# A block of S5 and attention on one core: other products between the last pairs, and x's store at another place in the queues

## The chip, the cores and the metric

The kernel runs on one core of a Trainium2 chip, as one launch. The metric is the device time of a whole execution in microseconds. A core has five engines, each with its own instruction queue: TensorE (PE in the profile; its weight loads are PEld), VectorE (DVE), ScalarE (ACT), GpSimd (POOL) and SyncE (SP), which here does little but start DMAs. Matrix products land in PSUM, eight banks of 128 x 512 f32; all else is in SBUF or in DRAM.

## The reference

Two layers run one after the other on x of shape (2, 2048, 512), each modulated by a condition vector of 512 per batch. The first is an S5 block: layer norm and modulation, a diagonal complex state space of 128 states scanned along the 2048 positions, a gated residual, and a feed-forward part. The second is multi-head attention (16 heads of width 32) whose layer norm takes its gain and offset from the condition.

```python
h = ln(y) * (1 + scale_a) + shift_a
y = y + gate_a * s5(h)                      # 2 Re(C scan(Lam, B h)) + D h
h = (ln(y) * (1 + scale_c) + shift_c) * (1 + scale_f) + shift_f
y = y + gate_f * (gelu(h @ W1 + b1) @ W2 + b2)
h = gamma(c) * (ln(y) * g + b) + beta(c)
q, k, v = split(h @ Wqkv.T + bqkv)
y = y + softmax(q k.T / sqrt(32)) v @ Wp.T + bp
```

W1 is 512 x 2048, W2 is 2048 x 512, Wqkv is 1536 x 512, all f32. (The sketch leaves out how the condition's shifts, scales and gates are made.)

## The kernel before

The kernel has a first part, up to about 1308 us, and then the attention. The first part walks through eight chunks of 512 rows, four of each batch, in the order `order`. Every chunk goes through the S5 layer, the feed-forward layer (ff) and the products for k, q and v; these are stored to DRAM (`kd`, `qd`, `vd`), and x with the bias of the output projection is stored to `x2` for the attention.

Chunk 0's ff is computed plainly: 16 hidden blocks, each `ff_first` (4 matmuls and a gelu) and `ff_second` (4 matmuls). In its shadow POOL makes, with `combine` (L784 to 796), the sums of weight blocks that a seven-product scheme (Strassen's in Winograd's form) needs, and SP stores them to DRAM as `w1d`, `w2d`, `wkd`, `wvd`. What is done beside which block is written down in a table `due`.

Chunks 1 to 7 are turns of a loop. In a turn, `now` is the chunk whose ff is computed, `behind` the one before it, whose q, k and v are made, and `ahead` the one after it, which goes through S5. The turn has four stretches on TensorE:

1. *ff pairs*: `pairs_of` with 8 pairs (products at L909). A pair is seven products of 4 matmuls, 128 x 256 each: 0, 1, 4, 2, then the previous pair's product 6, then 3 and 5. Between them, ScalarE copies a half bank (`za`, L926), VectorE makes sums (`za`, `zb`, L927 to L943), and ScalarE applies gelu (`hidden`). Then come the two input products of S5 for `ahead` (`s5_in`, `pu`, L530, 8 matmuls of 128 x 512 each).
2. *FF-out*: `whole_of` with depth 8 (L962), seven products of 32 matmuls in the order 0, 1, 2, 3, 5, 4, 6. After product 2 stand the output products of S5 (`s5_out`, `pa`, L576).
3. *q/k pairs*: `pairs_of` with 4 pairs, over sums of blocks that `at_sums` has POOL make (`parts`, L874 to 877).
4. *v*: `whole_of` with depth 2.

Work of the other engines is put between the products by lists: `beside[n]` is issued after step n of `pairs_of` (two steps a pair) or after product n of `whole_of`. The schedule is manual: each engine, and SP's DMA starting too, executes its instructions in the order in which the program issues them. An instruction that waits holds back all that follows it on its engine.

Some helpers are spread over those lists. `norm_steps` gives a layer norm as rows (statistics, L144, a row each), a scale (13 small VectorE operations, L149 to L133) and a normalisation (L154). `block_steps` gives a transpose in two steps: 32 x 32 turns on VectorE (L460), and a `move` of 16 DMAs on SP (L467). After the move ScalarE's `features` (L477) apply the modulation. `at_rows` (L625 to 634) adds the projection's bias to x's rows on POOL (L627) and stores them with four DMAs on SP (L634). `load_x` (L222) loads the rows of the chunk after `ahead`, into one of three buffers in rotation, which is the buffer of `behind`. `gated_in` (L1105 to 1116) adds FF-out's quarters to x, and `bias` (L1140) adds the second ff bias for `ahead`. `ff_features` are `ahead`'s features for the next turn's ff; one stands in each of the q/k pairs' steps 3 to 6.

Weights come through a ring of four 1 MB slots (`wk`, `wq`, `wv`, `w3`). `more` (L855 to 865) starts the next load on SP after a product has used a slot up; the stream is, a turn, eight loads of w1d, seven of w2d, four of wkd and two of wvd. Eight landing counters are used in rotation by the DMAs that an engine starts, so a DMA also waits for the one eight before it.

After the loop three weights are loaded again for the last chunk's v, k and q (`wkqv`, L1210 to 1214), which is computed plainly with the first heads' attention.

Of the kernel before, what the change touches and what calls it, by code (L numbers as in the profile page):

```python
# [8 lines left out]
F32 = mybir.dt.float32  # L9
# [30 lines left out]
def tile_s5_block_then_sln_attention(  # L40
# [482 lines left out]

    def s5_in(b, c):
        uT = fts.pop((b, c))
        bu = []
        for w in (bT_re, bT_im):
            pu = ones.tile([P, CH], F32, name="pu")
            for k in range(KC):
                nc.tensor.matmul(pu, w[:, k, :], uT[:, k, :], start=k == 0, stop=k == KC - 1)  # L530
            bu.append(pu)
        bus[b, c] = bu

# [78 lines left out]
    def ff_out(b, c):  # L612
        xc, po = xt[b, c], pos.pop((b, c))
        for t in range(TT):
            g = work1.tile([P, D], F32, name="gated")
            nc.vector.tensor_mul(g, po[:, t, :], gate[b, "gate_f"])
            nc.gpsimd.tensor_tensor(xc[:, t, :], xc[:, t, :], g, ALU.add)
# [165 lines left out]

    def combine(block, to, *shape):  # L784

        for at, tag in ((1, "hi"), (5, "lo")):
            pair = work1.tile([P, 2, HC], F32, name="sums", tag=tag)
            views = [pair[:, m, :].rearrange("p (k f) -> p k f", k=shape[0]) for m in range(2)]
            if at == 1:
                nc.gpsimd.tensor_tensor(views[1], block(1, 0), block(1, 1), ALU.add)  # L790
                nc.gpsimd.tensor_tensor(views[0], views[1], block(0, 0), ALU.subtract)
                s2 = views[0]
            else:
                nc.gpsimd.tensor_tensor(views[0], block(0, 0), block(1, 0), ALU.subtract)
                nc.gpsimd.tensor_tensor(views[1], block(0, 1), s2, ALU.subtract)
            nc.sync.dma_start(to(at, at + 2), pair)
# [20 lines left out]
    def by_rows_w2(q):  # L817

        def block(i, j):
            return w2_sb[j][:, q : q + 1, HC * i : HC * i + HC]  # L820

        def to(m0, m1):
            return w2d[m0:m1, :, q, :].rearrange("m p e -> p m e")

        combine(block, to, 1)

# [27 lines left out]

    def more():  # L855

        n = begun[0]
        if n == total:
            return
        begun[0] += 1  # L860
        tag = slots[n % 4]
        src, size = stream[n]
        w = (strip if tag == "w3" else wlate).tile([P, FH * HC], F32, name="wring", tag=tag)
        nc.sync.dma_start(w[:, :size], src)
        ready.append(w)
# [27 lines left out]
    def bank():  # L893
        return psq.tile([P, CH], F32, name="pp")

    def pairs_of(n, x, shape, take, beside):

# [21 lines left out]
        for c in range(n + 1):  # L919
            if c < n:  # L920
# [7 lines left out]
                product(p1, w, 4, t4, 0, True, False)  # L928
                product(p1, w, 2, t1, 1, False, False)
            if c:  # L930
                product(pps[c - 1][1], ws.pop(c - 1), 6, x22, 1, False, True)
                more()
                za, (_, p1) = zas.pop(c - 1), pps.pop(c - 1)
                nc.vector.tensor_tensor(za[:, 0, :], p1[:, HC:], za[:, 0, :], ALU.add)
                take(c - 1, 0, 1, za[:, 0, :])
# [14 lines left out]

    def whole_of(depth, weights, x, take, beside):

        a0, a1, b1, b0 = bank(), bank(), bank(), bank()
        u = strip.tile([P, CH], F32, name="u", tag="u")
        v = strip.tile([P, CH], F32, name="v", tag="v")
        z = strip.tile([P, CH], F32, name="z", tag="z")

        def product(m, out, start, stop):
# [8 lines left out]
            if last:  # L967
                more()

        def run(m):  # L970
            for what, *args in beside.get(m, ()):
                what(*args)

        product(0, a0, True, False)
        nc.scalar.copy(u, a0)
# [21 lines left out]
        take(0, 1, u)  # L997

    for i, now in enumerate(order[:1]):

# [30 lines left out]
        for n in range(3):  # L1031
            due[13, 1].append((more,))

# [20 lines left out]
    for i, now in enumerate(order):  # L1054
# [17 lines left out]

        beside = {n: [] for n in range(-1, 2 * FH + 2)}
        if ahead:
            rows, scale, to = norm_steps(*ahead)
            turns, move = block_steps(*ahead, tag_of(*ahead), by_way=True)
            if new:
                beside[0] += [(s5_gates, ahead[0])]
                beside[6] += [(gate_row, ahead[0], "gb2", gate_b2)]
            beside[0] += rows[:2]  # L1080
            beside[1] += rows[2:3]
            beside[2] += rows[3:]
            beside[4] += scale
            beside[6] += to[:2]
            beside[8] += to[2:]
            beside[10] += turns[:3]
# [68 lines left out]
        whole_of(FH, weight, operand, gated_in, beside)  # L1155
        blocked.pop(now, None)
# [22 lines left out]
        pairs_of(KC, parts_of["at"], 1, heads, beside)  # L1179
        if not ahead:  # L1180
            continue

        vw = [ready.pop(0), ready.pop(0)]

# [3 lines left out]

        parts = parts_of["at"]
        xv = {0: parts[0], 1: parts[1], 2: parts[2], 3: parts[3], 4: parts[4], 5: parts[5], 6: parts[6]}  # L1190

        def operand_v(m, q, t):
            return xv[m][:, q, 0, t * P : t * P + P]

# [667 lines left out]
```

## Time and profile before

Three runs took 3343.62, 3346.92 and 3352.35 us, median 3346.92.

| | us |
|---|---|
| profiled execution, its time | 3344.9 |
| its span, first to last instruction | 3343.0 |
| TensorE busy (mean granted clock 0.986) | 3192.0 |
| first part: start to the first pair | 0 to 212.88 |
| loop of seven turns | 212.88 to 1282.64 |
| last chunk's v, then attention | 1291.12 to 3343 |
| HBM traffic, mean over the span | 119 GB/s |

An entry of the profile names the line in the kernel, the engine, the operation, what is written from what is read, partitions x elements, and a count. Where an engine stood idle before it, brackets give for how long and which instruction or DMA ended that. SPq entries are SyncE's starting of DMAs, whose time includes waits in between when several are put together in one entry.

### The profile page before, as it was taken

The page shows a single profiled execution, that of the slowest core. Times are in us where ns is not written, and L with a number is a line of the kernel's source. Part 1 is how long each engine was busy: PE and PEld are TensorE (multiplying, and loading weights), DVE is VectorE, ACT ScalarE, POOL GpSimd, SP SyncE. Part 2 cuts the span into 40 slices and gives each one's busy share as a digit, 9 for nine tenths or more (in the row PEclk, how much of TensorE's full clock was granted, in tenths as well). Part 3 has the DMA queues.
Part 4 walks back from the last instruction along what each step waited for, and adds up shares of the span by engine and source line. Part 5 has one row for each costly group of instructions (what it writes and reads, how often), then busy time and mean ns, then how long its engine had stood idle before and what let it go on. Part 6 is the DMA issues. An engine that isn't in the chain of part 4 may idle for free.

```text
span 3343.0 us, 38784 instructions
## 1 busy us (share of the span) xinstructions
PE 3192.0 (95%) x12900; PEld 1771.2 (53%) x12900; DVE 2452.6 (73%) x3200; ACT 2014.8 (60%) x2391; POOL 2412.2 (72%) x1464
## 2 busy tenths in 40 slices
PE   7989999999999998999999999999999999999996
PEld 4457878777877885444444444444444444443432
DVE  5246565666657434788888888888888888888884
ACT  2111313121212122699999999999888988888862
POOL 2857363545445332599989999999999999999986
PEclk9999999999999999999999999999999999999998
DMA  8555656566574755323231323133243243233233
GB/s 302 180 191 177 211 182 210 184 202 207 175 228 157 220 188 188 103 62 73 69 73 48 74 67 74 50 76 77 59 99 87 68 97 86 74 85 84 66 101 96
DMA packets 298013, 422.19 MB, mean 126 GB/s; under 512 B 98712, under 2 KB 195224, under 8 KB 286678
## 3 DMA queue, kind: packets, MB, share of 16 engines
q1 hardware_dynamic: 297814, 419.72, 43.5%
q8 instruction: 102, 1.67, 0.2%
q14 instruction: 97, 0.79, 0.1%
HBM read 309.38 MB, written 87.94 MB: 119 GB/s over the span
## 4 chain that ended last, share of the span: by engine, by line
PE 46%; DVE 18%; ACT 17%; POOL 5%; issue 4%; DMA 3%; SPq 2%; ACTq 0%; DVEq 0%; POOLq 0%
PE pp L909 13%; PE o L1358 10%; PE s L1289 8%; DVE run L1305 8%; ACT x L1300 7%; PE pp L962 7%; ACT x L1348 5%; ACT pT L1348 4%; DVE pT L1343 3%; PE py L1441 3%; DVE run L1309 2%; SPq L467 2%; PE pu L530 1%; PE pt_run L1317 1%; PE pk L646 1%
## 5 line engine op out<-in xcount | busy, mean ns | idle before, releaser
L1337 POOL TENSOR_TENSOR x<-x,shift 128x1024 f32<-128x1024 f32 x704 | 1653.4, 2391 | 133.8 <-DMA shift<-flat 109.1
L1289 PE MATMUL s<-qs,ks 128*128 128x512 f32 x2688 | 823.4, 427 | 39.3 <-DVE run L1305 24.8
L1300 ACT COPY x<-s 128x1024 f32<-128x1024 f32 x704 | 692.0, 1011 | 141.6 <-PE s L1289 133.4
L1305 DVE TENSOR_TENSOR run<-s,run 128x1024 f32<-128x1024 f32 x576 | 705.0, 1224 | 74.6 <-ACT x L1300 29.0
L1348 ACT ACTIVATE x<-x 128x1024 f32<-128x1024 f32 x704 | 738.2, 1058 | 19.2 <-POOL x L1337 18.9
L1358 PE MATMUL o<-x,v 128*64 128x512 f32 x2816 | 717.8, 612 | 0.0
L1289 PEld LDWEIGHTS s<-qs,ks 128*128 128x128 f32 x2688 | 444.6, 189 | 454.4 <-DVE run L1305 155.8
L1343 DVE TENSOR_TENSOR pT<-s,shift 128x1024 f32<-128x1024 f32 x320 | 388.8, 1215 | 50.3 <-PE s L1289 50.3
L1309 DVE TENSOR_TENSOR run<-s,run 128x1024 f32<-128x1024 f32 x320 | 389.1, 1216 | 9.5 <-PE s L1289 8.9
L1348 ACT ACTIVATE pT<-pT 128x1024 f32<-128x1024 f32 x320 | 339.4, 1061 | 76.5 <-DVE pT L1343 76.3
L909 PE MATMUL pp<-parts,wring 128*128 128x256 f32 x1344 | 329.8, 389 | 16.1 <-POOL parts L875 15.4
L1358 PE MATMUL o<-pT,v 128*64 128x512 f32 x1280 | 329.3, 593 | 6.6 <-ACT pT L1348 6.6
L1358 PEld LDWEIGHTS o<-x,v 128*64 128x64 f32 x2816 | 157.2, 136 | 309.4 <-issue 250.6
L962 PE MATMUL pp<-wring,h 128*128 128x256 f32 x1344 | 293.3, 379 | 0.0
L909 PEld LDWEIGHTS pp<-parts,wring 128*128 128x128 f32 x1344 | 261.8, 196 | 57.5 <-POOL parts L875 17.8
L909 PE MATMUL pp<-fT,wring 128*128 128x256 f32 x1008 | 251.2, 382 | 26.7 <-DVE zb L943 17.4
L962 PEld LDWEIGHTS pp<-wring,h 128*128 128x128 f32 x1344 | 255.6, 190 | 39.6 <-issue 5.7
L909 PEld LDWEIGHTS pp<-fT,wring 128*128 128x128 f32 x1008 | 190.3, 191 | 60.4 <-DVE zb L943 23.0
L1070 POOL TENSOR_TENSOR h<-h 128x256 f32<-128x256 f32 x56 | 42.5, 758 | 230.2 <-ACT h L1068 218.8
L1358 PEld LDWEIGHTS o<-pT,v 128*64 128x64 f32 x1280 | 91.3, 137 | 191.3 <-issue 141.1
L1305 DVE TENSOR_TENSOR run<-s,x 128x1024 f32<-128x1024 f32 x64 | 78.4, 1225 | 121.6 <-ACT x L1300 121.6
L477 ACT ACTIVATE fT<-moved,s_shift,s_scale 128x512 f32<-128x512 f32 x28 | 20.5, 803 | 217.3 <-DMA moved<-fT 153.8
(360 smaller groups left out, 3173.2 us busy)
## 6 DMA issues: line engine op xcount, KB each, us to landing
wring<-w1d SPq DMA_DIRECT2D x56, 896.0 KB
wring<-w2d SPq DMA_DIRECT2D x49, 1024.0 KB
ks<-kd SPq DMA_DIRECT2D x128, 256.0 KB
qs<-qd SPq DMA_DIRECT2D x512, 64.0 KB
shift<-flat SPq DMA_DIRECT2D x64, 512.0 KB
wring<-wkd SPq DMA_DIRECT2D x28, 896.0 KB
moved<-fT SPq DMA_DIRECT2D x224, 64.0 KB
x<-in_x SPq DMA_DIRECT2D x8, 1024.0 KB
```

Source lines behind the costliest of these rows:

```text
L467: nc.sync.dma_start(moved[32 * g : 32 * g + 32, :, a * P : (a + 1) * P], turned[32 * a : 32 * a + 32, :, g, :],)
L909: nc.tensor.matmul(to, w[:, m, k, :], moving, start=start and k == 0, stop=stop and k == 1, skip_group_check=True,)
L962: nc.tensor.matmul(out[:, t * HC : t * HC + HC], x(m, q, t), w[:, q, :], start=start and q == 0 and t == 0, stop=stop and q == depth - 1 a ...
L1289: nc.tensor.matmul(s[:, e, :], kst[pair_of[n], e][:, kt * P : (kt + 1) * P], qst[n][:, e, :], start=True, stop=True,)
L1300: nc.scalar.copy(x, s)
L1305: nc.vector.tensor_tensor(runs[n], s, kept[n, 0] if kt == 1 else runs[n], ALU.max)
L1309: nc.vector.tensor_tensor(runs[n], raw_scores(n, kt), runs[n], ALU.max)
L1337: nc.gpsimd.tensor_tensor(x, x, shifts[n], ALU.add)
L1343: nc.vector.tensor_tensor(x, s, shifts[n], ALU.add)
L1348: nc.scalar.activation(x, x, AF.Exp)
L1358: nc.tensor.matmul(outs[n][64 * e : 64 * e + 64, :], v[:, kt, e : e + 2, :], x[:, e, :], start=first, stop=final,)
L1441: nc.tensor.matmul(py, o4[:, g, :], wp[:, g, :], start=g == 0, stop=g == NG - 1)
```

## The change

Nothing in the arithmetic's outcome is meant to differ, and the attention isn't touched. The edits are these.

1. `pairs_of` takes a `bridge`: work that is issued between product 5 of the last pair and its product 6. In the ff pairs it is the first of the two products of `s5_in`, which now can be issued in two parts. In the q/k pairs it is the first product of v's `whole_of`, which is split into `whole_of` (first product) and `rest_of`.
2. The layer norm of `ahead` for S5: its rows move from the turn's ff pairs to the previous turn's v (for chunk 2, into chunk 0), and scale, normalisation, turns, move, direct rows come four or so steps earlier; the features move from step 14 to 13. The rows of `behind`'s norm move later, and its scale into step 15.
3. In FF-out, `behind`'s turns move from product 1 to product 2 and alternate with `s5_out`; `at_sums` comes after product 3 instead of 4; `at_rows` and `load_x` come after product 5's normalisation and bias, where before they stood after products 1 and 3. `ahead`'s move is issued after both.
4. In chunk 0 the first three ring loads are started by ScalarE, after hidden block 14's first half, instead of by SP; half of w2's sums and half of `ff_out` go to another engine.
5. The three weights that are loaded again are loaded inside the last turn's q/k pairs.

```diff
-    def s5_in(b, c):
+    def s5_in(b, c, parts=(0, 1)):
...
     def ff_out(b, c):
         for t in range(TT):
+            if t % 2:
+                g = work1.tile([P, D], F32, name="hid", tag=f"hid{t // 2}", bufs=1)
+                nc.scalar.copy(g, po[:, t, :])
+                nc.gpsimd.tensor_tensor(g, g, gate[b, "gate_f"], ALU.mult)
+            else:
...
-        combine(block, to, 1)
+        combine(block, to, 1, engine=nc.vector if q % 2 else nc.gpsimd)
...
-    def more():
+    def more(engine=nc.sync):
-        nc.sync.dma_start(w[:, :size], src)
+        engine.dma_start(w[:, :size], src)
...
-    def pairs_of(n, x, shape, take, beside):
+    def pairs_of(n, x, shape, take, beside, bridge=()):
...
                 product(p1, w, 2, t1, 1, False, False)
+            if c == n:
+                for what, *args in bridge:
+                    what(*args)
             if c:
                 product(pps[c - 1][1], ws.pop(c - 1), 6, x22, 1, False, True)
                 more()
...
-    def whole_of(depth, weights, x, take, beside):
-        a0, a1, b1, b0 = bank(), bank(), bank(), bank()
+    def whole_of(depth, weights, x):
+        a0 = bank()
...
+        product(0, a0, True, False)
+        return product, a0
+
+    def rest_of(begun, take, beside):
+        product, a0 = begun
+        a1, b1, b0 = bank(), bank(), bank()
...
         for n in range(3):
-            due[13, 1].append((more,))
+            due[14, 0].append((more, nc.scalar))
+        later[order[2]] = norm_steps(*order[2])
+        due[10, 1] += later[order[2]][0]
...
-            rows, scale, to = norm_steps(*ahead)
+            rows, scale, to = later.pop(ahead)
...
-                beside[6] += [(gate_row, ahead[0], "gb2", gate_b2)]
-            beside[0] += rows[:2]
-            beside[1] += rows[2:3]
-            beside[2] += rows[3:]
-            beside[4] += scale
-            beside[6] += to[:2]
-            beside[8] += to[2:]
-            beside[10] += turns[:3]
-            beside[11] += turns[3:] + move
-            beside[12] += [(s5_direct, *ahead)]
-            beside[14] += [(s5_features, *ahead, k) for k in range(KC)]
+                beside[4] += [(gate_row, ahead[0], "gb2", gate_b2)]
+            beside[0] += scale
+            beside[2] += to[:2]
+            beside[4] += to[2:]
+            beside[6] += turns[:3]
+            beside[7] += turns[3:] + move
+            beside[8] += [(s5_direct, *ahead)]
+            beside[13] += [(s5_features, *ahead, k) for k in range(KC)]
+            bridge += [(s5_in, *ahead, (0,))]
...
-            beside[3 + 2 * n] += b_rows[n : n + 1]
-        pairs_of(FH, parts_of["ff"], TT, hidden, beside)
+            beside[(5, 9, 11, 12)[n]] += b_rows[n : n + 1]
+        beside[15] += b_scale
+        pairs_of(FH, parts_of["ff"], TT, hidden, beside, bridge)
...
-        for what, *args in b_scale:
-            what(*args)
         if ahead:
-            s5_in(*ahead)
+            s5_in(*ahead, (1,))
             s5_turn(*ahead)
...
-        beside[1] += b_to + [(at_rows, *behind)] + b_turns + b_move
+        beside[1] += b_to
...
-            for t in range(TT):
+        for t in range(TT):
+            if ahead:
                 beside[2] += [(s5_out, *ahead, t)]
+            beside[2] += b_turns[t : t + 1]
+        beside[2] += b_move
         beside[3] += [(fourth, 0), (fourth, 1)]
         beside[3] += [(at_features, *behind, k) for k in range(KC)]
-        if i + 2 < len(order):
-            beside[3] += [(load_x, *order[i + 2])]
+        beside[3] += [(at_sums, *behind)]
         if ahead:
             beside[3] += rows + scale
             beside[5] += to + [(bias, t) for t in range(TT)]
             beside[4] += turns + move
-        beside[4] += [(at_sums, *behind)]
-        whole_of(FH, weight, operand, gated_in, beside)
+        beside[5] += [(at_rows, *behind)]
+        if i + 2 < len(order):
+            beside[5] += [(load_x, *order[i + 2])]
+        rest_of(whole_of(FH, weight, operand), gated_in, beside)
...
+        def begin_v():
+            vw.extend((ready.pop(0), ready.pop(0)))
+            vw.append(whole_of(2, weight_v, operand_v))
+        def reload(name, tag, src):
+            w = wlate.tile([P, KC, D], F32, name=name, tag=tag)
+            nc.sync.dma_start(w, src.rearrange("(k p) f -> p k f", p=P))
+            again[name] = w
...
+        if not ahead:
+            beside[2].append((reload, "wv", "wq", w_vT))
+            beside[4].append((reload, "wk", "wv", w_kT))
+            beside[2 * KC].append((reload, "wq", "wk", w_qT))
+        pairs_of(KC, parts, 1, heads, beside, [(begin_v,)] if ahead else [])
...
-        whole_of(2, weight_v, operand_v, values_in, {})
-    wkqv = []
-    for name, src in (("wv", w_vT), ("wq", w_qT), ("wk", w_kT)):
-        w = wlate.tile([P, KC, D], F32, name=name)
-        nc.sync.dma_start(w, src.rearrange("(k p) f -> p k f", p=P))
-        wkqv.append(w)
-    wv, wq, wk = wkqv
+        beside = {}
+        if i + 2 < len(order):
+            later[order[i + 2]] = norm_steps(*order[i + 2])
+            beside = dict(zip((0, 2, 3, 5), ([row] for row in later[order[i + 2]][0])))
+        rest_of(vw[2], values_in, beside)
+    wk, wq, wv = (again[n] for n in ("wk", "wq", "wv"))
```

More of the change, by code (lines that the diff above doesn't have):

```diff
@@ L522, in s5_features @@
         features(b, c, k, u_scale, mod[:, SHIFT_A], tag_of(b, c))
-    def s5_in(b, c):
-        uT = fts.pop((b, c))
-        bu = []
-        for w in (bT_re, bT_im):
+    def s5_in(b, c, parts=(0, 1)):
+        for i in parts:
+            w = (bT_re, bT_im)[i]
             pu = ones.tile([P, CH], F32, name="pu")
             for k in range(KC):
-                nc.tensor.matmul(pu, w[:, k, :], uT[:, k, :], start=k == 0, stop=k == KC - 1)
-            bu.append(pu)
-        bus[b, c] = bu
+                nc.tensor.matmul(pu, w[:, k, :], fts[b, c][:, k, :], start=k == 0, stop=k == KC - 1)
+            bus.setdefault((b, c), []).append(pu)
+        if 1 in parts:
+            fts.pop((b, c))
     def s5_turn(b, c, other=nc.gpsimd):
@@ L614, in ff_out @@
         for t in range(TT):
-            g = work1.tile([P, D], F32, name="gated")
-            nc.vector.tensor_mul(g, po[:, t, :], gate[b, "gate_f"])
+            if t % 2:
[3 more added lines that the diff above has]
+            else:
+                g = work1.tile([P, D], F32, name="gated")
+                nc.vector.tensor_mul(g, po[:, t, :], gate[b, "gate_f"])
             nc.gpsimd.tensor_tensor(xc[:, t, :], xc[:, t, :], g, ALU.add)
@@ L782, in rows_of_biases, with combine @@
         along_rows(bp_row, [vec[:, V_BP + k : V_BP + k + 1] for k in range(KC)], ones, None)
-    def combine(block, to, *shape):
+    def combine(block, to, *shape, engine=nc.gpsimd):
         for at, tag in ((1, "hi"), (5, "lo")):
@@ L789, in combine @@
             if at == 1:
-                nc.gpsimd.tensor_tensor(views[1], block(1, 0), block(1, 1), ALU.add)
-                nc.gpsimd.tensor_tensor(views[0], views[1], block(0, 0), ALU.subtract)
+                engine.tensor_tensor(views[1], block(1, 0), block(1, 1), ALU.add)
+                engine.tensor_tensor(views[0], views[1], block(0, 0), ALU.subtract)
                 s2 = views[0]
             else:
-                nc.gpsimd.tensor_tensor(views[0], block(0, 0), block(1, 0), ALU.subtract)
-                nc.gpsimd.tensor_tensor(views[1], block(0, 1), s2, ALU.subtract)
+                engine.tensor_tensor(views[0], block(0, 0), block(1, 0), ALU.subtract)
+                engine.tensor_tensor(views[1], block(0, 1), s2, ALU.subtract)
             nc.sync.dma_start(to(at, at + 2), pair)
@@ L949, in pairs_of @@
             run(2 * c + 1)
-    def whole_of(depth, weights, x, take, beside):
-        a0, a1, b1, b0 = bank(), bank(), bank(), bank()
-        u = strip.tile([P, CH], F32, name="u", tag="u")
-        v = strip.tile([P, CH], F32, name="v", tag="v")
-        z = strip.tile([P, CH], F32, name="z", tag="z")
+    def whole_of(depth, weights, x):
+        a0 = bank()
         def product(m, out, start, stop):
@@ L968, in product @@
                 more()
+        product(0, a0, True, False)
[3 more added lines that the diff above has]
+        a1, b1, b0 = bank(), bank(), bank()
+        u = strip.tile([P, CH], F32, name="u", tag="u")
+        v = strip.tile([P, CH], F32, name="v", tag="v")
+        z = strip.tile([P, CH], F32, name="z", tag="z")
         def run(m):
@@ L972, in run @@
                 what(*args)
-        product(0, a0, True, False)
         nc.scalar.copy(u, a0)
@@ L997, in whole_of @@
         take(0, 1, u)
+    later = {}
     for i, now in enumerate(order[:1]):
@@ L1073, in tile_s5_block_then_sln_attention @@
         beside = {n: [] for n in range(-1, 2 * FH + 2)}
+        bridge = []
         if ahead:
-            rows, scale, to = norm_steps(*ahead)
+            rows, scale, to = later.pop(ahead)
             turns, move = block_steps(*ahead, tag_of(*ahead), by_way=True)
@@ L1178, in tile_s5_block_then_sln_attention @@
             beside[2 * KC].append((ff_sums, *ahead, nc.gpsimd))
[L1179 to L1183, printed above, removed]
+        parts = parts_of["at"]
+        vw = []
         def weight_v(m):
@@ L1187, in weight_v @@
             return w[:, m % 4], m in (3, 6)
-        parts = parts_of["at"]
-        xv = {0: parts[0], 1: parts[1], 2: parts[2], 3: parts[3], 4: parts[4], 5: parts[5], 6: parts[6]}
         def operand_v(m, q, t):
-            return xv[m][:, q, 0, t * P : t * P + P]
+            return parts[m][:, q, 0, t * P : t * P + P]
+        def begin_v():
[5 more added lines that the diff above has]
+            again[name] = w
+        again = {}
+        if not ahead:
[3 more added lines that the diff above has]
+        pairs_of(KC, parts, 1, heads, beside, [(begin_v,)] if ahead else [])
+        if not ahead:
+            continue
         def values_in(e, half, src):
```

## The prediction

> **What bounds the kernel now.** I read the shares of busy time first, then the waits of TensorE in the seven-product loop, then the time line of its second turn (chunk 2). In the first fence are the two heads: TensorE's share of the span, and the loop (212.88 to 1282.64 us) with the busy time of each engine, PEclk and DMA share.
>
> ```profile
> PE 3192.0 (95%) x12900; PEld 1771.2 (53%) x12900; DVE 2452.6 (73%) x3200; ACT 2014.8 (60%) x2391; POOL 2412.2 (72%) x1464
> ...
> 212.88:1282.64 1069.76, 1030.02 (x4488) 854.48 (x4488) 636.66 (x1138) 229.32 (x429) 507.20 (x414) 0.99 0.61 193
> ```
>
> TensorE is busy 1030.02 of the loop's 1069.76 us, so at most 39.7 us of idling (and some half-clock time counted as busy) can be won there; the other engines are no bound by sum, only by order. The attention from 1308 us on isn't edited. The waits of TensorE in the loop and at both its ends: line, what it waited for, total us, times, longest.
>
> ```profile
> PE pp L909 <- DVE zb L943: 17.4, 14, 1.2
> PE pp L909 <- POOL parts L875: 15.4, 6, 2.7
> PE pp L909 <- DMA wring<-w1d: 9.2, 1, 9.2
> PE pv L658 <- DMA wv<-in_w_vT: 8.5, 1, 8.5
> PE pu L530 <- ACT fT L477: 3.3, 6, 0.9
> PE pa L576 <- DVE gated L579: 2.8, 5, 0.8
> ```
>
> Each is small and is paid once a turn. Now one turn: time, duration, operation, [idle before, releaser]. TensorE, then POOL, ScalarE and SyncE:
>
> ```profile
> 428.71 7.07 PE L962 MATMUL pp<-wring,h 128*128 128x256 f32 x32
> 484.75 1.03 PE L909 MATMUL pp<-fT,wring 128*128 128x256 f32 x4
> 488.50 4.69 PE L909 MATMUL pp<-parts,wring 128*128 128x256 f32 x12 [2.72 <-POOL parts L875]
> 495.61 2.75 PE L909 MATMUL pp<-parts,wring 128*128 128x256 f32 x12
> ```
>
> ```profile
> 446.77 5.56 POOL L627 TENSOR_TENSOR x<-x,bp_row 128x512 f32<-128x512 f32 x4 [0.72 <-DVE xn L154]
> 475.12 1.50 POOL L1115 TENSOR_TENSOR z<-z,gate_f 128x512 f32<-128x512 f32 x1 [7.87 <-DVE z L987]
> 476.70 1.33 POOL L1116 TENSOR_TENSOR x<-x,z 128x512 f32<-128x512 f32 x1
> 477.99 5.33 POOL L1140 TENSOR_TENSOR x<-x,gb 128x512 f32<-128x512 f32 x4
> ```
>
> ```profile
> 468.24 2.93 ACT L477 ACTIVATE fT<-moved,s_shift,s_scale 128x512 f32<-128x512 f32 x4 [31.79 <-DMA moved<-fT]
> 502.81 0.80 ACT L477 ACTIVATE fT<-moved,z_shift,z_scale 128x512 f32<-128x512 f32 x1
> 503.51 0.35 ACT L926 COPY za<-pp 128x256 f32<-128x256 f32 x1
> ```
>
> ```profile
> 452.35 2.86 SPq L634 DMA_DIRECT2D x<-x  x4
> 455.31 11.31 SPq L467 DMA_DIRECT2D moved<-fT  x16
> 467.80 0.42 SPq L222 DMA_DIRECT2D x<-in_x  x1
> 471.13 7.23 SPq L864 DMA_DIRECT2D wring<-wkd  x2
> 482.80 10.26 SPq L467 DMA_DIRECT2D moved<-fT  x16
> ```
>
> To see: x's rows are done and stored early (446.77 to 458), 30 us before anything needs SP again; the q/k pairs wait 2.72 us for block sums and then run 12 matmuls in 4.69 us instead of 2.75; ahead's first ff feature (502.81) is the instruction just before the third pair's copy (503.51) in ScalarE's queue. I call the start of the first FF-out product, 428.71, T0; a matmul of 256 columns has a pitch of 0.216 us, so a product of a pair takes 0.864, a pair 6.05, an FF-out product 6.91.
>
> **Gains, part by part.** The loop has six turns with a chunk ahead.
>
> *Block sums before the z gate.* The q/k pairs' wait goes: 484.75 + 0.86 to 488.50 is 2.89, and half clock after it 4.69 − 2.75 = 1.94; 4.8 × 6 = 28.8. POOL's four sums (1.26 each) run when the features are there, T0+42 to 47.8, seven us before the pairs.
>
> *Bridge in the q/k pairs.* 14 waits on zb of 1.24, of which 6 stand before v; 1.24 plus a slow first row of some 0.2 is 1.5. Eight matmuls at 0.216 (1.73) cover it: 9.0.
>
> *Bridge in the ff pairs.* The same 9.0. But the four s5 features move ahead of the last pair's copy in ScalarE's queue; ScalarE gives them 2.93 us, the copy falls to 417.5 and VectorE's za to 418.4, where TensorE would want it at 416.9 (all by chunk 2's clock): −1.6 × 6. Net −0.5. The wait of pu on features (0.58 to 0.93, one of them with half clock) goes: 6.5.
>
> *s5_out and turns interleaved*: pa's gated wait, 0.56 and a slow row, 0.83 × 5 = 4.2.
>
> *Start.* The first three ring loads left SP at 206.61, behind w2d stores that waited on POOL, and the pair began at 212.88 after 9.17 of idling. On ScalarE they can leave near 195 to 199; but the third waits there for the counter of the first (landing about 204), and the last gelu stands behind it, as chunk 2's four norm rows (3.3) ahead of it on VectorE put it back too; against that, half of w2's sums and half of chunk 0's output products leave POOL's and VectorE's queues for the other engine. I take 4, ends 0 and 10. The row of the loads' own issue is 1.42 us for three. The Trainium skill's page "DMA: Bandwidth & Descriptors", section "Issuing engines are not separate DMA queues", says another issuing engine only saves issue time on the sequencer; taken alone, that makes this term 1.4 at most and the sum 2.6 higher, but here the queue's wait, not the issue, is what 206.61 shows.
>
> *End.* wv's wait of 8.47 goes, and the pv group ran 15.79 for 32 × 0.432 = 13.8; k and q loads behind it move up. I take 10 (8.5 to 10.6).
>
> Gains: 28.8 + 9.0 − 0.5 + 6.5 + 4.2 + 4 + 10 = 62.
>
> Other moved work I cost at nothing. ahead's norm rows (four of 0.84 us) on VectorE go to the v phase, where it is idle in gaps over 1 us; without that cover, up to 3.4 a turn. b_scale's 13 tiny operations took 8.7 us beside a busy POOL (421.53 to 430.27) and move under the last pair. Ahead's scale, turns, move and direct rows of the ff pairs come some four slots earlier, beside pairs whose VectorE and POOL have gaps as long. The eighth w1d load now stands behind 16 moves on SP: by issue pitches it lands some 0.2 us before its pair (0 to 0.5 a turn).
>
> **The loss: x's rows and store at the end of FF-out.** In the changed order POOL does: block sums, z gate, x add, bias, *rows*, then v and u; SP does: x store (4, waiting for the rows), load_x, the third wkd, ahead's 16 moves, the fourth wkd. load_x takes the buffer that the stores read, so SP stands in it until they have landed. Rows end (call it R) by steps: the behind chunk's turns end after pa, T0+29.1; 16 moves × 0.644 = 10.3 and a landing of 2.05, T0+41.5; features 2.93 beside the sums, sums to T0+47.8; z, held by VectorE's scale operations (2.2 us with POOL idle, up to 8.7 with POOL busy, which the sums make it), T0+49.6; gate and add 2.8; bias 5.33; rows 5.1: R = T0+62.9. Bounds: uncontended scale 60.9, fully contended 64.5.
>
> Behind R: store issue and landing 6.4 (452.35 to 458.66 in the landing records), then load_x and wkd, FIFO, 2.3 to 2.7 us each once running and 4.9 for one alone: the third wkd lands at R+13.8. The moves, each also waiting for the DMA eight before it, land by R+20.5. First ff feature 0.8, copy 0.35, za 0.42 and hand-overs: the third pair's product 3 can start at R+22.3. It is due at T0+70.8 (pairs from 55.2; 5.19 + 6.05 + 4.32). So a turn loses R − 48.5 = 14.4 us. Before, the moves had landed at 494.55 for a feature at 502.81: 8.1 us of slack, and now none. TensorE stops twice: 9.3 us for the load, then some 2.2 for the feature, after which I charge 1.5 of half clock. The nearest row is the 1.94 after 2.72 us of idling, where the granted clock was 0.58.
>
> The Trainium skill's page "TensorE: Matmul & The Clock Gate", section "Part 1: The HAM clock gate (the "warmup" mystery)", has the clock halved only after an idle window of about 3.4 us. By it the second stop would cost no ramp, and the sum were 9 lower, 3367; the trace's row at 488.50 halves after 2.72, and I go by the row.
>
> Five turns lose 15.9: 79.5. The sixth has no load_x: R − 53.1 + 1.5 = 11.3. Together 91; ends 70 (R 60.9, no half clock) and 104 (R 64.5, slow landings).
>
> **Sum.** 3344.9 (span 3343.0 + 1.9 around it) − 62 + 91 = 3373.9 on the profiled run's scale. The median shown, 3346.92, is 2.0 above that run, so I say 3376, 0.9% slower. A change below 0.3% (10 us) can't be told from none.
>
> **Rivals.**
> *B, the store is hidden (faster).* If rows end before T0+50 the moves land in time, nothing stops, and the time is 3346.9 − 62 = 3285. One point decides: R. For it: POOL is busy 507 of 1070 us and has gaps (7.87 before z). Against: sums can't start before T0+42, and sums, gate, bias and rows are 18 us of one queue.
> *C, half hidden.* R is at 60.9 and SP's chain a few us shorter than from isolated rows (stores landing in 4): the loss is 55 to 70, the time 3340 to 3355, no difference to be told at its middle.
> *D, slower still.* ScalarE's loads hold the last gelu and the start gains nothing (+4), w1d comes 0.5 late in six turns (+3), and rows wait for a fully contended scale (+13): 3396.
> *E, the bridges do nothing.* If pu or v's first product has no free PSUM bank, TensorE waits in the bridge instead: 18 less gain, 3394. Against it: six banks, of which v's first product needs one.
>
> **Chances.** Mine 0.60, with its own range 3360 to 3392; B 0.07; C 0.18; D and E 0.15. Slower: 0.60 + 0.15 is 0.75, less 0.02 for mine's lower edge: 0.73. C gives 0.13 to same and 0.05 to faster, so same is 0.15, and faster 0.12 with B. The range runs from the lower half of mine and C's upper part, 3347, to D and E, 3395; below it stand B and C's lower part.
>
> **What would show it.** Right: TensorE waits at the third q/k pair of turns 1 to 5, put down to wring<-wkd and then to L926/L927's za, 10 us or more together; x<-x stores issued near T0+63; no wait on parts; zb waits gone but at the end of the last turn. Wrong: rows done by T0+55, or load_x issued without standing still behind the stores, or the third wkd already landed when its pair begins. If the q/k pairs still wait for parts, the gain falls by up to 28.8.

## The result and the profile after

The changed kernel takes 3396.14 us (median of 3392.54 to 3399.36) against 3347.91 before: 1.44% slower, ratio 1.0144, 95% interval 1.0126 to 1.0161. The profiled execution is one of 3395.7 us, its span 3393.8, against 3344.9 and 3343.0. The difference between the two spans is 50.8 us; 29 had been forecast, and the measured time lies 1.1 us above the forecast range.

From the heads of the profile after, the shares of busy time, and the windows view of the loop (217.47 to 1338.85 us):

```profile
PE 3196.7 (94%) x12900; PEld 1777.5 (52%) x12900; DVE 2390.7 (70%) x3214; ACT 2017.6 (59%) x2393; POOL 2394.0 (71%) x1450
...
217.47:1338.85 1121.38, 1034.14 (x4485) 860.47 (x4485) 564.88 (x1129) 230.90 (x429) 501.58 (x418) 0.97 0.58 183
```

TensorE has hardly more busy time in the loop: 1034 against 1030 us, at a mean granted clock of 0.97 instead of 0.99. The loop is 52 us longer, and 47.5 of these are idle time. TensorE's main waits from the first pair to the end of the loop (line, releaser, total, times, longest):

```profile
PE pp L914 <- DMA wring<-wkd: 49.5, 10, 9.5
PE pp L914 <- DVE za L932: 30.2, 13, 7.6
PE pp L914 <- ACT hid L617: 10.6, 1, 10.6
PE pp L967 <- DVE z L1002: 4.7, 4, 1.3
PE pp L914 <- DVE zb L951: 2.5, 2, 1.2
```

All that the change was to remove is gone: 15.4 us on parts, 12 of the 14 waits on zb, the waits of pu and pa. In its place stand 49.5 us on the ring's wkd loads and 30.2 on za, neither of which was a wait of note before. Turn 2 of the loop, where T0, the start of FF-out, is now 442.03. TensorE, POOL, SyncE, ScalarE:

```profile
491.64 7.17 PE L967 MATMUL pp<-wring,h 128*128 128x256 f32 x32 [1.15 <-DVE z L1002]
498.65 1.03 PE L914 MATMUL pp<-fT,wring 128*128 128x256 f32 x4
499.52 2.75 PE L914 MATMUL pp<-parts,wring 128*128 128x256 f32 x12
...
519.53 2.04 PE L914 MATMUL pp<-fT,wring 128*128 128x256 f32 x4 [9.49 <-DMA wring<-wkd]
521.37 3.65 PE L914 MATMUL pp<-parts,wring 128*128 128x256 f32 x12
...
528.46 1.13 PE L914 MATMUL pp<-fT,wring 128*128 128x256 f32 x4 [2.58 <-DVE za L932]
...
531.98 1.13 PE L914 MATMUL pp<-fT,wring 128*128 128x256 f32 x4 [1.53 <-DMA wring<-wkd]
```

```profile
491.67 1.50 POOL L1134 TENSOR_TENSOR z<-z,gate_f 128x512 f32<-128x512 f32 x1 [1.43 <-DVE z L1002]
...
494.54 5.31 POOL L1157 TENSOR_TENSOR x<-x,gb 128x512 f32<-128x512 f32 x4
499.81 4.94 POOL L632 TENSOR_TENSOR x<-x,bp_row 128x512 f32<-128x512 f32 x4
```

```profile
504.78 2.86 SPq L639 DMA_DIRECT2D x<-x  x4
511.14 0.40 SPq L222 DMA_DIRECT2D x<-in_x  x1
511.63 0.45 SPq L869 DMA_DIRECT2D wring<-wkd  x1
512.19 12.96 SPq L467 DMA_DIRECT2D moved<-fT  x16
525.25 0.53 SPq L869 DMA_DIRECT2D wring<-wkd  x1
```

```profile
526.88 0.81 ACT L477 ACTIVATE fT<-moved,z_shift,z_scale 128x512 f32<-128x512 f32 x1 [14.34 <-DMA moved<-fT]
527.60 0.35 ACT L931 COPY za<-pp 128x256 f32<-128x256 f32 x1
```

The q/k pairs start without a wait at 498.65, and run at full clock (12 matmuls in 2.75 us instead of 4.69). Then they stop. POOL ends the rows at 504.75, T0+62.7; SP starts the x store only then, stands 3.5 us until it has landed, starts load_x and at 511.63 the third wkd load; in the kernel before, that load left 22.6 us or more before its pair's turn, in each of the six turns. TensorE waits 9.49 us for it. ahead's moves come next, ScalarE waits 14.34 us for them, and the copy behind the feature (527.60) is what TensorE's second wait, on za, stands on. The fourth load is late by 1.53 as well.

The span, cut at the starts of the stretches on TensorE, against the terms of the prediction (changes in us, summed over the turns):

| stretch | forecast | measured |
|---|---|---|
| start to the first pair | −4 | +4.6 |
| ff pairs and pu, 7 turns | −6.0 | −6.9 |
| FF-out with pa, 7 turns | −4.2 | +1.5 |
| q/k pairs and v, turns 1 to 6 | +53.2 | +58.1 |
| last q/k pairs, and last v to the first scores | −10 | −8.6 + 2.0 |
| sum | +29 | +50.7 |

### The profile page after: what moved, and what is told of

Its sections match the earlier page's. It is cut to its first block, busy times and chain, and to the rows that moved or that the text cites. A ratio compares the mean times of both kernels' runs of the same rounds, so it can differ in the third digit from the quotient of the medians.

```text
span 3393.8 us, 38792 instructions
## 1 busy us (share of the span) xinstructions
PE 3196.7 (94%) x12900; PEld 1777.5 (52%) x12900; DVE 2390.7 (70%) x3214; ACT 2017.6 (59%) x2393; POOL 2394.0 (71%) x1450
## 3 DMA queue, kind: packets, MB, share of 16 engines
q10 hardware_dynamic: 432, 2.75, 0.2%
## 4 chain that ended last, share of the span: by engine, by line
PE 48%; ACT 17%; DVE 15%; DMA 8%; POOL 5%; SPq 3%; issue 3%; ACTq 0%; DVEq 0%; POOLq 0%
PE pp L914 11%; PE o L1390 9%; PE pp L967 8%; PE s L1321 7%; ACT x L1332 7%; DVE run L1337 7%; ACT x L1380 5%; ACT pT L1380 3%; DVE pT L1375 2%; DMA wring<-wkd 2%; POOL x L1369 2%; PE py L1473 2%; DVE run L1341 2%; SPq L467 2%; PE pu L529 2%
## 5 line engine op out<-in xcount | busy, mean ns | idle before, releaser
L1375 DVE TENSOR_TENSOR pT<-s,shift 128x1024 f32<-128x1024 f32 x320 | 388.6, 1214 | 49.6 <-PE s L1321 49.6
L914 PE MATMUL pp<-fT,wring 128*128 128x256 f32 x1008 | 262.0, 393 | 93.2 <-DMA wring<-wkd 49.5
```

The source lines that it names most:

```text
L914: nc.tensor.matmul(to, w[:, m, k, :], moving, start=start and k == 0, stop=stop and k == 1, skip_group_check=True,)
L1375: nc.vector.tensor_tensor(x, s, shifts[n], ALU.add)
```

## The experiments

Theory Q is the prediction's: what costs is the place of the x store in SP's queue, with the third and fourth wkd loads and ahead's moves behind it. Its rivals are other parts of the change.

**Rows, store and load_x put back, on the changed kernel.**

```diff
-        beside[1] += b_to
+        beside[1] += b_to + [(at_rows, *behind)]
...
+        if i + 2 < len(order):
+            beside[3] += [(load_x, *order[i + 2])]
         beside[3] += [(at_sums, *behind)]
...
-        beside[5] += [(at_rows, *behind)]
-        if i + 2 < len(order):
-            beside[5] += [(load_x, *order[i + 2])]
```

> Only edit: x's rows and store go back behind product 1's normalisation and load_x behind product 3's features; all else is as in the changed kernel. Theory Q (the third and fourth wkd loads and ahead's moves stand on SP behind the x store, which stands behind POOL's rows): the stretch of q/k pairs and v falls in each of six turns from 51.4-54.9 us to about 36.3 (before's 42.5 less 4.8 and 1.5), 6 x 15.8 = 95, so about 3301 us; no wait on wring<-wkd, none over 1.3 on za. Rival N (the delay comes from other moved work: ahead's norm rows in v, the features at step 13, the late norm of behind): the wkd waits stay for the most part and the time stays above 3370.

Measured 3308.23 us, ratio to before 0.9889 (0.9873 to 0.9906): 88 us faster than the changed kernel by the medians, 84 when each is set against the runs of the kernel before beside it. It is also faster than before, and 7 us above the 3301 expected. Its main waits in the loop:

```profile
PE pp L914 <- ACT hid L617: 10.6, 1, 10.6
PE pp L914 <- DVE za L932: 9.3, 8, 2.3
PE pp L967 <- DVE z L1002: 3.5, 3, 1.2
PE pp L914 <- DVE zb L951: 2.5, 2, 1.2
PE pp L914 <- DMA wring<-wkd: 2.4, 4, 0.8
```

49.5 on wkd became 2.4, and 30.2 on za became 9.3 (six of these waits are the features', 0.95 to 1.22 each, in the ff pairs). In turn 1 q/k and v take 36.31 us, against 51.71 in the changed kernel and 42.49 before. Over six turns this stretch falls by 88.0 us. So, beside the other edits, the move costs 84 to 88, and these other edits together gain 36 to 40.

**The same move alone, on the kernel before.** In `whole_of`'s lists of the kernel before, `at_rows` and `load_x` go from `beside[1]` and `beside[3]` to the end of `beside[5]`; nothing else.

> The kernel before with one edit only: x's rows, store and load_x moved behind the bias, as the change has them. The formula of the prediction: bias ends at T0+54.6, rows 5.0 more, R = T0+59.6; the block sums, here behind the rows on POOL, come 5.0 later too, so the q/k pairs wait 7.7 for parts instead of 2.7; the third pair's product 3 starts at R+22.3 = T0+81.9 against 75.9. 5 to 8 us a turn, 35 to 45 in all, about 3385. If the loss of the changed kernel came from the move together with something else that the change has (the sums ahead of z, late turns), it is below 15 here.

Measured 3394.14 us, ratio 1.0137 (1.0120 to 1.0154): the move alone slows the kernel before by 47 us, more than the 35 to 45 expected. The waits from its first pair on:

```profile
PE pp L909 <- POOL parts L875: 44.7, 6, 7.6
...
PE pp L909 <- DVE za L927: 9.9, 5, 3.1
...
PE pp L909 <- DMA wring<-wkd: 4.1, 4, 1.8
```

Here POOL's part of the move shows by itself: the block sums stand behind the rows, and the wait on parts went from 15.4 to 44.7 us, 4.9 more a turn. Behind this wait, the moves and the loads are less late than in the changed kernel. A turn's q/k and v stretch grew by 8.4 to 9.5 us, in the sixth by 5.6.

The parts of the change don't add up, then. The move costs 47 us alone and 84 to 88 beside the other edits; and while the rows are late, all the other edits together gain nothing (3394 without them, 3396 with them). The time by which the rows end sets when the q/k pairs can go on, so what those edits save ahead of that is waited away again: turn 2 ends 106.9 us behind T0 with the move alone and 109.1 in the changed kernel, against 98.7 in the kernel before.

**Rows late on POOL, but last on SP.** `at_rows` and `load_x` go from `beside[5]` to `beside[6]`, so on SP behind both wkd loads and ahead's moves.

> Only edit: x's rows, store and load_x are issued after product 6, so on SP behind the third and fourth wkd loads and ahead's moves; POOL does the rows as late as in the changed kernel or later. Theory Q1 (what matters is the order on SP): as with the rows put back, about 3301 to 3312, x's store issued near T0+64. Rival Q2 (POOL's rows themselves, in front of the last gates and the next sums, cost it): less than half of the 95 comes back, above 3350.

Measured 3358.26 us, ratio 1.0039 (1.0024 to 1.0054). By its number this is rival Q2's, above 3350 and with less than half of the 95 us back, but the waits are not the ones that Q2 named. Of the waits on wkd 1.2 us are left, and another has come:

```profile
PE pp L967 <- DMA wring<-wvd: 31.3, 5, 7.6
PE pp L914 <- DVE za L932: 13.7, 7, 7.1
```

SP starts the x store at 505.69 and load_x at 513.69, again standing until the store has landed. Now the kd stores and the first wvd load stand behind that, and v waits up to 7.6 us a turn for it. The queue's stop hasn't gone; it has been moved to its next customer.

**load_x alone later.** `load_x` to `beside[6]`, the store where the change has it.

> Only edit: load_x is issued after product 6, the x store stays in front of the third wkd load. Theory L (SP's standing in load_x until the stores have landed, and load_x's own 1 MB ahead of wkd, are a main part): the third wkd leaves some 3.5 us earlier and lands 6 earlier, 20 to 30 us in five turns, about 3368 to 3376. Rival: turn 6 of the changed kernel has no load_x and still lost as much as the others (+8.82), so 0 to 10 us, 3386 to 3396.

A single run: 3384.68 us, 11 less than the changed kernel, where 20 to 30 and 0 to 10 were the two expectations. The third wkd load is waited for 7.0 us instead of 9.5, the copy behind the features for 2.36 instead of 2.58 (both in turn 2), and in five turns v now waits 2.0 to 2.6 for wvd. load_x is a small part; the store's wait for the rows is the large one.

**The store started by POOL.** The x store's four DMAs, and `load_x` after product 6, are started by GpSimd; the rows stay late.

> On top of the changed kernel: x's rows stay late, but the x store is started by POOL, and load_x by POOL too, after product 6; so nothing on SP waits for the rows. Theory Q (the loss is SP's queue standing behind the x store): the waits on wring<-wkd and on wvd go, the q/k and v stretch falls from 52 to about 37 a turn, 3305 to 3320. Rival P (POOL's late rows cost it, with SP or without): the stretch stays above 45, 3360 or more.

A single run: 3342.57 us, 54 less than the changed kernel. That lies between the theories: the q/k and v stretch fell to 40 us in turns 1, 2, 4 and 6 and to 44 in turn 5 (36.3 to 37.9 with the rows put back), but stayed at 53 in turn 3, where the changed kernel takes 55. Of the waits on wkd 2.0 us are left, so most of the loss, 54 of 84 to 88 us, was SP's queue. What is left in turn 3 comes over POOL. From the time line of turn 3, POOL and ScalarE:

```profile
644.85 4.94 POOL L632 TENSOR_TENSOR x<-x,bp_row 128x512 f32<-128x512 f32 x4
650.09 2.21 POOL L639 DMA_DIRECT2D x<-x  x4 [0.30 <-POOL x L632]
...
658.34 0.80 POOL L222 DMA_DIRECT2D x<-in_x  x1 [3.42 <-DMA x<-x]
659.16 1.27 POOL L1134 TENSOR_TENSOR u<-u,gate_f 128x512 f32<-128x512 f32 x1
```

```profile
660.46 0.59 ACT L181 COPY gate_f<-pt_ar 128x512 f32<-128x512 f32 x1 [27.66 <-POOL u L1134]
660.95 0.38 ACT L931 COPY za<-pp 128x256 f32<-128x256 f32 x1
```

In turn 3 the batch changes and ScalarE writes a new `gate_f` row, ahead of the first pair's copy. It must wait for the old row's last reader, u's gate, which stands on POOL behind the rows; TensorE waits 14.00 us for that. In this run the store and `load_x`, which POOL starts, stand ahead of that gate too: it begins at T0+71.0, against T0+64.7 in the changed kernel, where TensorE's wait is 7.62. So the 14.00 are not the price of the rows alone. In every turn ahead's 16 moves took 13.4 to 14.3 us to start, beside the x store and load_x, where they take 10.3 to 11.5 with the rows put back.

**The start.** Two runs: w2's sums all on POOL, on the changed kernel (`combine(block, to, 1)` without the engine); and the whole end of chunk 0 as before (sums, loads on SP, output rows), on the kernel with the rows put back.

> Only edit: all of w2's sums are on POOL again; ring loads on ScalarE and the split output rows stay. Theory V (VectorE stands in the w2 sums until their buffers are stored, 11.1 + 7.2 + 3.6 us of idling, and so block sums and output rows of chunk 0 come late): the first pair starts at 208 to 213 us instead of 217.5, 5 to 9 us less, about 3389. Rival A (the early ring loads take the DMA engines from the w2d stores): POOL then stands as long on the same buffers, but VectorE doesn't; the pair starts no earlier than 216.

> On top of the kernel with x's rows put back (median 3308.2): chunk 0's end as it was before, that is w2's sums all on POOL, the three ring loads on SP, output rows as before. Theory S (the new end of chunk 0 costs 4.6 us of start and 1.0 of half clock, and has no part that gains): the first pair starts at 212.9, 5 to 6 us less, about 3302. Rival: some of its parts gain (loads already landed), and what is lost by putting those back cancels it: 3306 to 3310.

With the sums on POOL the first pair begins at 212.53 instead of 217.47, which is theory V. The time was 3394.43, a single run: the last q/k pairs begin 5.0 us earlier too, but what follows them, where this edit changes nothing, took 3.9 us longer in this run. VectorE's queue at the start of the changed kernel shows the cause:

```profile
195.69 0.42 DVE L795 TENSOR_TENSOR sums<-w,w 128x256 f32<-128x256 f32 x1 [11.09 <-DMA w2d<-sums]
...
209.52 0.49 DVE L795 TENSOR_TENSOR sums<-w,w 128x256 f32<-128x256 f32 x1 [3.55 <-DMA w2d<-sums]
...
212.00 0.68 DVE L879 TENSOR_TENSOR parts<-fT 128x512 f32<-128x512 f32 x1
...
216.11 0.69 DVE L621 TENSOR_TENSOR gated<-po,gate_f 128x512 f32<-128x512 f32 x1 [0.71 <-ACT hid L617]
```

VectorE stands in the sums until the buffers of earlier sums have been stored. Chunk 1's block sums, at 196.94 before, come at 212.00, and the output rows that free chunk 0's PSUM banks after them. The same two in the kernel before, and its first pair; then the first pair of the changed kernel:

```profile
196.94 1.05 DVE L874 TENSOR_TENSOR parts<-fT 128x512 f32<-128x512 f32 x1 [17.94 <-PE ph L594]
...
211.49 0.69 DVE L616 TENSOR_TENSOR gated<-po,gate_f 128x512 f32<-128x512 f32 x1 [0.53 <-POOL x L617]
...
212.88 2.05 PE L909 MATMUL pp<-fT,wring 128*128 128x256 f32 x4 [9.17 <-DMA wring<-w1d]
```

```profile
217.47 2.08 PE L914 MATMUL pp<-fT,wring 128*128 128x256 f32 x4 [10.59 <-ACT hid L617]
```

Part of such differences arises earlier: chunk 0's last hidden block begins anywhere from 191.5 to 194.7 us in the traces of this case. Counted from there, the first pair begins after 19.6 us in the kernel before and 24.1 in the changed one (23.5 to 24.5 in five other kernels with the same chunk 0). With the sums on POOL it is 20.6 and 20.8 in two kernels. So half the sums on VectorE cost 3.3 to 3.5 us, and the rest of the new start still gains nothing.

With the whole end of chunk 0 as before, the first pair began at 216.38, not at 212.9, and the time was 3304.47 (0.9879, 0.9863 to 0.9896), 3.8 less than without it, with intervals that overlap. Counted from the last hidden block the pair begins after 22.0 us, 2.2 earlier than with only the rows put back. The last output row, which frees the last bank, ended at 216.25; chunk 2's norm rows still stand on VectorE in chunk 0 there, and the last product of chunk 0 began 1.7 us later. In the kernel before that last row ended at 212.18 and the pair began at 212.88: the banks were free just 0.7 us before the loads landed.

**Features at the copy.** On the kernel with the rows put back, with w2's sums on POOL:

```diff
                 nc.scalar.copy(za[:, 0, :], p0[:, :HC])
+                if c == n - 1:
+                    run("copied")
...
-            beside[13] += [(s5_features, *ahead, k) for k in range(KC)]
+            beside["copied"] += [(s5_features, *ahead, k) for k in range(KC)]
```

> On top of the kernel with x's rows put back: w2's sums all on POOL, and ahead's four S5 features issued right behind the last ff pair's copy instead of before it. Theory F (the features' 2.9 us of ScalarE in front of the copy hold TensorE 1.22 a turn and a slow row): the wait on za in the last ff pair goes in six turns, 1.6 x 6 = 9.6, and the start gains 5 as it did alone: about 3294. Rival: the features end too late for the bridge, TensorE waits as long at pu: only the start's 5, 3303.

Measured 3296.09 us, ratio 0.9851 (0.9837 to 0.9866), 12 less than with the rows alone put back. The ff pairs' sum fell by 8.4 us, and the first pair came 4.7 earlier (214.19 against 218.85; 3.5 counted from the last hidden block). So the features' place cost 1.4 a turn (the prediction had 1.6).

**wq's load later, and the scale later.** In the kernel with the rows put back: the reload of wq is started behind the first ks and qs loads, and FF-out's `scale` goes from `beside[3]` to the front of `beside[5]`.

> On top of the kernel with x's rows put back, two edits in separate stretches: the reload of wq is started behind the first ks and qs loads; in FF-out ahead's norm scale comes after z instead of before. Theory W (wq's 1 MB ahead of ks and qs in the DMA queue holds the first scores): v's first product to the first score falls from 21.2 us by 2.5 to 5. If starting DMAs on SP is the bound there, by 0.5. Theory Z (the 13 small operations beside a busy POOL delay z, for which product 6 waits 1.2): those waits go, FF-out falls by 1.2 to 1.6 in each turn that has one, 4 to 6 in all. Together 6 to 10, about 3300; rival to Z: ahead's moves come later and the third q/k pair waits for the features instead, 0 to -10.

Measured 3315.26 us, ratio 0.9909 (0.9895 to 0.9924): 7 slower than without the two, though the two profiled executions are only 1.7 apart. Both gained where they were meant to and lost more elsewhere. Product 6's waits went and FF-out fell by 4.4, but ahead's turns and moves came later, and q/k and v rose by 9.0 (5.7 us on wkd in place of 2.4). From v's first product to the first score it took 5.2 us less, and 4.3 was given back at once: TensorE waited 4.39 for ScalarE's vt rows soon after.

**Sums after z.** On the kernel with the features at the copy: `at_sums` goes from `beside[3]` to the front of `beside[5]`, between z's gate and the bias, and the third ring load of chunk 0 behind the last gelu.

```diff
-        beside[3] += [(at_sums, *behind)]
+        beside[5] += [(at_sums, *behind)]
...
-        for n in range(3):
+        for n in range(2):
             due[14, 0].append((more, nc.scalar))
+        due[15, 0].append((more, nc.scalar))
```

> On top of the kernel with the features at the copy (median 3296.1): behind's block sums stand on POOL between z's gate and the bias instead of ahead of the gate, and the third ring load of chunk 0 leaves ScalarE behind the last gelu instead of ahead of it. Theory Z2 (z is late because the scale's 13 small operations run beside POOL's sums): without POOL beside them they take 2.2 us, product 6 doesn't wait (3.5 in e6, with the slow rows 4 to 5), and the sums still end by T0+56.4, so the q/k pairs wait 0 to 0.5. Theory G (the third load on ScalarE stands until the first has landed, and the last gelu behind it): the 5.1 on hid goes, 3 to 6. Together about 3287. Rival: z's gate moves POOL beside the scale all the same and the sums come late, 3294 to 3300.

Measured 3289.69 us, ratio 0.9828 (0.9814 to 0.9843). Both theories hold: no wait on z, FF-out 4.3 less, the wait on hid in front of the last output product 2.5 instead of 5.1 and the first pair at 209.53 instead of 214.19 (after 18.0 us instead of 20.6, counted from the last hidden block; 18.6 in the next run, which starts alike). The q/k and v stretch takes 36.31 us in every turn but the third, which rose to 42.54, with TensorE waiting 4.27 for the first za behind the copy into `gate_f`.

**The gate row later.** On top of that, `gate_row(…, "gate_f", …)` moves from the end of FF-out to `beside[7]` of the q/k pairs.

> On top of the kernel with the sums after z (median 3289.7): in turn 3, where the batch changes, the row of gate_f is written in the middle of the q/k pairs instead of ahead of them. Theory U (ScalarE's copy into gate_f waits for POOL's last reader of the old one, u's gate, which stands behind the rows and the bias, and holds the first pair's copy): the stretch of turn 3 falls from 42.5 us to 36.3, the wait of 4.3 on za goes, about 3283. Rival: the copy waits as long there, or holds the bank that the features need: 3287 to 3292.

Measured 3284.01 us, ratio 0.9813 (0.9796 to 0.9829): 1.9% faster than before, and the best of these. Turn 3 takes 37.20. Its waits of TensorE from chunk 0's end to the last v:

```profile
PE pp L914 <- ACT hid L617: 4.7, 1, 4.7
PE pp L914 <- DVE zb L953: 2.5, 2, 1.2
PE pp L914 <- DVE za L934: 0.8, 2, 0.5
```

## Why the prediction was wrong, and where it was right

The direction and the mechanism were right; the size was 22 us short by the spans, 20 by the medians.

*The chain behind R* held to about a microsecond. z's gate began at T0+49.6 (forecast 49.6), the rows ended at T0+62.7 (62.9), the third pair began at T0+77.5 (the load forecast to land at 76.7), its product 3 at T0+86.4 (85.2). The rows put back are worth 84 to 88 us, where the prediction charged 91. Two sizes inside were off and, by luck, made up for each other. The second wait, 2.58, brought no half clock in this turn, for which 1.5 had been charged; and the fourth wkd load's 1.53 had not been. By the Trainium skill's page "TensorE: Matmul & The Clock Gate", section "Part 1: The HAM clock gate (the "warmup" mystery)", a stop this short leaves the clock alone, which is what this row shows. It isn't what turn 6 shows, where the granted clock fell to a half at 1192.18, 1.2 us behind a stop of 2.65 at the same place. The prediction had gone by the row of before, and 3367, its sum by the page, was further off still. Turn 6, without load_x, was charged 4.6 less than the others. It lost as much as they did in the stretch (14.8 us between the changed kernel and the one with the rows put back, against 13.5 to 15.5): the store's wait, not load_x, was the price.

*Block sums before the z gate and the bridge in the q/k pairs*, 4.8 and 1.5 a turn: the stretch fell by 6.2 to 6.6 in every turn whose other waits were out of the way (42.49 to 36.31 in turn 1), and the sum over six turns in the last experiment is 37.2 against 37.8. Right.

*The bridge in the ff pairs and pu*: right, −6.9 for −6.0, and the price of the features ahead of the copy was right too (1.4 a turn against 1.6).

*The start* is the step that failed by most: "I take 4, ends 0 and 10" against a loss of 4.6, 8.6 us apart. Two things were missed. The wait on the w1d load was read as the whole obstacle, although the output rows that free the banks ended 0.7 us before it, so that earlier loads alone could have won no more than that. And moving half of w2's sums to VectorE was counted as relief for POOL. Those sums wait for their own buffers' stores; on VectorE that wait holds back the block sums and the output rows. No loss was among the ends. Part of the 4 was there to be had, with the sums on POOL and the third load behind the last gelu: counted from the last hidden block, the last two experiments begin the first pair after 18.0 and 18.6 us, where the kernel before and the one with the move alone, whose starts are alike, took 19.6 and 18.9.

*FF-out*: −4.2 against +1.5. pa's wait went, but the prediction used the contended scale only to place R. The same late z holds product 6, which accumulates into the bank that z reads, 1.1 to 1.3 us in four turns, with a slow first matmul behind each (four matmuls take 1.13 us instead of 1.03). The last two experiments took that out, and their FF-out is 4.2 and 5.1 below that of the kernel before.

*q/k and v*: 4.9 above the forecast, in turns 3 and 6. The forecast was +9.6 to before in turns 1 to 5 and +5.0 in turn 6; turn 3 lost 12.4, turn 6 lost 8.8, and the others 8.8 to 9.8. Turn 3 has the wait that the run with POOL's store shows, and the prediction had no term for it. ScalarE in turn 3 of the changed kernel:

```profile
677.42 0.59 ACT L181 COPY gate_f<-pt_ar 128x512 f32<-128x512 f32 x1 [20.91 <-POOL u L1134]
677.90 0.38 ACT L931 COPY za<-pp 128x256 f32<-128x256 f32 x1
```

TensorE waits 7.62 us for this copy in the first pair, 20 us before the moves hold it again for 5.48. Rows on POOL ahead of u's gate are one more way in which the move reaches TensorE.

*The end*: −6.6 for −10. wv's wait went, but the first scores then waited 5.47 for qs. The lower bound took SP's ks and qs loads to move up with v; they stand behind the last pair's qd stores and the 1 MB load of wq (starting that load later gave 5.2 us there), and the first scores begin at 1359.18, half a microsecond after the last of those 16 issues (1342.64 to 1358.66).

The rivals: B needed rows before T0+50, and C rows at T0+60.9 with a shorter chain on SP; they ended at T0+62.7, and both fell with that. E did not happen. D named the start without gain, a late w1d load and a fully contended scale. Of these the first happened, and was worse than none; the loop waits 0.3 us for w1d, and the rows came before the T0+64.5 of a fully contended scale. That D's 3396 is the measured time is luck.

## What to carry to other kernels

A late producer on one engine costs little until a queue that serves others stands on it: before a store is put behind slow work, list what its queue starts next, with the time by which each is due. Such a stop can't be cured by moving it down the same queue, as the loads next in line inherit it; let the producer come early, as it did before. Work handed to an idle engine brings its waits with it, and a wait that is removed uncovers the next one, which here was 0.7 us behind.

## What the runs showed of the hardware that was not expected

A stop of TensorE of 2 to 3 us may or may not halve its clock. In the kernel before, a stop of 2.72 us was followed by half clock. At the first za of turn 3, the same place in two runs that differ only in chunk 0, a stop of 2.32 us was followed by half clock and one of 2.31 was not: four matmuls took 1.89 and 1.13 us. First the kernel with the rows put back, then the same with chunk 0's end as before:

```profile
643.89 1.89 PE L914 MATMUL pp<-fT,wring 128*128 128x256 f32 x4 [2.32 <-DVE za L932]
```

```profile
640.61 1.13 PE L914 MATMUL pp<-fT,wring 128*128 128x256 f32 x4 [2.31 <-DVE za L932]
```

What decides it can be read from the granted clock. In each trace it changes only on a grid of 3.413 us, whose phase differs from run to run. Here are two neighbouring slots of that grid, again for the two kernels (start and end, length, busy time of TensorE, its weight loads, VectorE, ScalarE and POOL, then the granted clock and DMA):

```profile
640.70:644.11 3.41, 1.09 (x6) 0.64 (x5) 0.42 (x1) 0.86 (x2) 3.04 (x3) 1.00 0.52 105
644.11:647.53 3.42, 3.42 (x9) 2.71 (x9) 0.01 (x1) 0.00 (x0) 0.00 (x0) 0.50 0.52 105
```

```profile
636.85:640.26 3.41, 1.45 (x7) 0.95 (x5) 0.12 (x1) 0.86 (x2) 3.33 (x3) 1.00 0.52 106
640.26:643.68 3.42, 3.07 (x14) 2.73 (x15) 1.30 (x3) 0.48 (x1) 0.29 (x1) 1.00 0.51 103
```

The stop of 2.32 lies whole in one slot, and the next slot is at 0.50. The one of 2.31 is split by the grid, 1.96 and 0.35, and nothing follows. In the loops of the thirteen traces all 48 stops that fill 2.0 us or more of one slot are followed by half clock; of the 141 stops over 1 us that fill less, four are (stops that begin at half clock are left out). Of the 26 stops of 2.0 to 3.1 us, 14 are. A plan doesn't know the phase of the grid, so a price for half clock after such a stop has to be a chance times about 2 us (1.94 behind the 2.72), and not a fixed term. The page on the clock gate named above, in the same section, says that the activity window of about 3.4 us runs free, so that its phase matters; that fits these records, but its threshold of a whole idle window does not fit a halving after 2.32.
